# An RWKV block on one core: six block projections by seven products each, and a variance in the unused strip of another matmul

## The chip, the core and the metric

The kernel runs on one core of a Trainium2 chip. The core has TensorE (PE, matrix products into PSUM; its weight loads are listed apart as PEld), VectorE (DVE), ScalarE (ACT), GpSimd (POOL), and SyncE (SP), which here issues nearly all DMAs. The metric is the time of one execution in microseconds of the device, as the median of several runs. A lower number is better.

## The reference

There are 8 batches of 256 tokens (T) with 512 channels (E), in 32 heads of 16. Everything is float32. The part that matters:

```python
xn = _ln(x, ln1_w, ln1_b);  sx = _token_shift(xn, state[:, i1])
xxx = tanh((xn + sx * maa_x) @ maa_w1);  x5 = xn + sx * (maa_stack + xxx @ maa_w2)
w = exp(-exp(time_decay + tanh(x5[1] @ decay_w1) @ decay_w2))
r, k, v = x5[3] @ Wr.T, x5[0] @ Wk.T, x5[2] @ Wv.T;  g = silu(x5[4] @ Wg.T)
def step(s, rkvw):                      # over the 256 tokens
    a = k_t[..., None] * v_t[..., None, :]
    out = einsum('bhk,bhkd->bhd', r_t, u * a + s);  return a + w_t[..., None] * s, out
att = ((a4 - m) * rsqrt(var + EPS)).reshape(b, l, E) * gn_w + gn_b   # per head
x = x + att * g @ Wo.T
xn2 = _ln(x, ln2_w, ln2_b);  sx2 = _token_shift(xn2, state[:, i0])
xk = xn2 + sx2 * ffn_maa_k;  xr = xn2 + sx2 * ffn_maa_r
x = x + sigmoid(xr @ ffn_Wr.T) * (square(relu(xk @ ffn_Wk.T)) @ ffn_Wv.T)
```

## The kernel before

Each batch passes three stages: `inputs_of_scan` (normalize, shift, mix, project to k, v, r, g and the decay w), `scan`, and `rest` (normalize per head, output projection `o`, second normalization, and the three projections of the feed-forward part: `fk`, `fr`, `fv`). Most tiles hold channels on the 128 partitions and tokens along the free axis, two blocks of 128 channels to a tile, so 512 channels are two tiles, called halves here (q = 0, 1 in the code).

The scan of a batch has four channel blocks of four tiles of 128 x 1024 each. For every tile a DMA spreads v over the partitions (`vs`, six buffers), DVE multiplies it by k (L864) and runs the recurrence (L866), POOL multiplies by r (L869), and PE gathers the sums over the state (L877). DVE adds the result to `att` (L883). That is 128 tiles over all batches, and the scans of the batches follow each other almost without a break; the projections of the batches before and after lie beside them.

All matmuls of projections are issued by the helper `mul` (L330), as one 128-column matmul for each block of contraction or as four of 32 columns side by side in the array. `project` gives channels on the partitions, `project_tokens` tokens. A whole projection is a product of 512 x 512 by 512 x 256. In the trace every float32 matmul instruction makes two records.

After the scan, `rest` squares `att` (L895), and PE averages the squares of each head (L903): four matmuls into four column strips of one tile. ACT turns the variance into its inverse root by a logarithm and an exponential (L908, L910). The 32 heads' values must then be spread over 128 partitions. In batches 0 to 6 ACT does it by sixteen copies of 32 rows (L932); in batch 7 PE does it by a matmul with a 0/1 matrix (L918). `att` is multiplied by it (POOL, L934; in batch 7 DVE, L926), scaled by `gn_w` and `gn_b` on ACT (L938) and multiplied by g (L943; in batch 7 L941). The output projection follows, and DVE adds it to x (L949). After the second normalization (L493, L467, L499, transposed by PE at L525) come `fk`, `fr` and `fv`; in batch 7 the last 256 columns of the result are made in two pieces of 128 (L983, L985), each sent out by its own DMA.

The strip matmul at L741 is part of `inputs_of_scan`: in the four 32-column strips of the array, strips 0 and 1 compute the decay's hidden layer, and strips 2 and 3 compute the hidden layer of the fifth mix twice, since its `tanh` (L749) is wanted on all partitions.

The weights of `o`, `fk`, `fr` and `fv` are loaded again for every batch, each as two tiles of the pool `Ws` (four buffers). PSUM has six buffers for matmuls (`ps`) and one wide one (`wrep`).

The order of all instructions is not that of the code. Every operation is recorded in a plan, and a long list of numbers (`ORDER`) says in which order they are emitted; each engine then runs its instructions strictly in that order. Buffers are given out along the list too.

Of the kernel before, what the change touches and what calls it, by code (L numbers as in the profile page):

```python
# [11 lines left out]
P = 128  # L12
# [24 lines left out]
C_SEL = C_SUM + P  # L37
NCONST = P + C_SEL + 2 * P

# [21 lines left out]

class Op:


    def __init__(self, engine, us, outs, ins, emit, mode):
        self.engine, self.us, self.emit, self.mode, self.narrow, self.table = engine, us, emit, mode, False, None
        self.bufs = list(dict.fromkeys([*outs, *ins]))
        self.before, self.wire = [], 0


class Plan:
# [1024 lines left out]
```

## Time and profile before

| | |
|---|---|
| median of 3 runs | 602.61 us (601.87 to 603.97) |
| profiled execution | 603.54 us, its span 601.7 us, mean TensorE clock 0.996 |
| matmuls and weight loads | 8308 each |
| DMA | 128.07 MB, 211 GB/s of HBM traffic over the span |

The span runs from the first to the last instruction in the profile. The granted clock is the share of TensorE's full clock that the throttle let pass. Groups of instructions are listed with their count, their busy time, the mean duration of one in ns, and the engine's idle time before them.

### The profile page before, as it was taken

How to read it: one execution, taken by the hardware profiler on the slowest of the kernel's cores; microseconds unless marked ns; L12 is line 12 of the kernel's file. 1: busy time of each engine (PE TensorE's matmuls, PEld its weight loads, DVE VectorE, ACT ScalarE, POOL GpSimd, SP SyncE). 2: the span in 40 equal slices, each digit the busy share in tenths (PEclk: the TensorE clock that was granted, in tenths of full speed). 3: DMA queues.
4: the chain of work that ended last, by engine and by line, in shares of the span. 5: the costliest groups of instructions: out<-in, count | busy, mean ns of one | idle time of the engine just before them, and what ended most of it. 6: DMA issues, size and time to landing. Idle time of an engine off the chain costs nothing.

```text
span 601.7 us, 19771 instructions
## 1 busy us (share of the span) xinstructions
PE 592.1 (98%) x8308; PEld 343.5 (57%) x8308; DVE 537.5 (89%) x500; ACT 504.9 (84%) x1198; POOL 507.2 (84%) x390
## 2 busy tenths in 40 slices
PE   8999998999999999999999999999999999999997
PEld 7575556457536775366553754465645574455464
DVE  5799999999999999899889999999999999996342
ACT  5898779899999999989999988989987879964531
POOL 0689999899989999999979898999798999888030
PEclk9999999899999999999999999999999999999999
DMA  8797768887888869778888897687899887952533
GB/s 295 228 246 196 186 155 246 239 221 203 224 229 246 221 163 276 220 203 230 203 250 221 224 251 212 163 234 206 219 257 242 214 234 206 280 180 73 189 122 109
DMA packets 55497, 128.07 MB, mean 213 GB/s; under 512 B 6112, under 2 KB 13680, under 8 KB 55408
## 3 DMA queue, kind: packets, MB, share of 16 engines
q1 hardware_dynamic: 51040, 122.61, 74.9%
q10 hardware_dynamic: 4368, 4.20, 2.2%
q8 instruction: 65, 1.06, 0.8%
q14 instruction: 24, 0.20, 0.1%
HBM read 118.39 MB, written 8.40 MB: 211 GB/s over the span
## 4 chain that ended last, share of the span: by engine, by line
PE 83%; POOL 10%; ACT 2%; DVE 2%; issue 2%; DMA 0%; SPq 0%; POOLq 0%; ACTq 0%
PE ps L330 70%; PE ps L877 8%; POOL st L869 5%; POOL mix L701 3%; PE ps L741 2%; PE ps L525 2%; POOL vs L861 1%; DVE st L493 1%; POOL rk L814 1%; PE ps L903 1%; DMA sq<-in_x 0%; POOL mix L569 0%; PE ps L819 0%; POOL att L833 0%; POOL mix L729 0%
## 5 line engine op out<-in xcount | busy, mean ns | idle before, releaser
L866 DVE TENSOR_TENSOR_SCAN st<-wrep,vs 128x1024 f32<-128x1024 f32 x128 | 288.2, 2277 | 2.2 <-POOL mix L701 0.6
L869 POOL TENSOR_TENSOR st<-st,r 128x1024 f32<-128x1024 f32 x128 | 254.7, 2002 | 8.3 <-DVE st L866 5.1
L864 DVE TENSOR_TENSOR vs<-vs,ps 128x1024 f32<-128x1024 f32 x125 | 147.7, 1208 | 6.1 <-ACT vs L857 4.1
L330 PE MATMUL ps<-Ws,mix 128*32 128x512 f32 (+3 forms) x836 | 115.5, 585 | 0.0
L330 PEld LDWEIGHTS ps<-Ws,mix 128*32 128x32 f32 (+1 forms) x836 | 39.0, 118 | 61.9 <-issue 54.6
L701 POOL TENSOR_TENSOR mix<-mix,xn 128x512 f32<-128x512 f32 x62 | 67.1, 1095 | 7.1 <-DVE mix L695 4.1
L330 PE MATMUL ps<-mix,Wv 128*32 128x256 f32 (+1 forms) x880 | 62.2, 389 | 2.1 <-POOL mix L701 2.1
L877 PE MATMUL ps<-st,con 128*32 128x256 f32 x1024 | 61.9, 380 | 0.0
L330 PE MATMUL ps<-mix,Wr 128*32 128x256 f32 (+1 forms) x760 | 60.7, 380 | 0.2 <-ACT v L772 0.2
L330 PE MATMUL ps<-mix,Wg 128*32 128x256 f32 (+1 forms) x904 | 60.4, 379 | 0.0
L330 PE MATMUL ps<-mix,Wk 128*32 128x256 f32 (+1 forms) x856 | 59.5, 380 | 0.0
L330 PE MATMUL ps<-mix,Ws 128*32 128x256 f32 (+1 forms) x928 | 57.5, 379 | 0.0
L330 PE MATMUL ps<-Ws,g 128*32 128x512 f32 (+1 forms) x464 | 56.9, 592 | 0.5 <-POOL g L943 0.5
L569 POOL TENSOR_TENSOR mix<-mix,xn 128x512 f32<-128x512 f32 x44 | 47.5, 1091 | 7.3 <-ACT mix L567 7.3
L330 PEld LDWEIGHTS ps<-mix,Wv 128*32 128x32 f32 (+1 forms) x880 | 39.8, 117 | 22.0 <-issue 4.4
L330 PEld LDWEIGHTS ps<-mix,Wr 128*32 128x32 f32 (+1 forms) x760 | 39.5, 119 | 17.2 <-issue 1.1
L827 ACT COPY att<-ps 32x256 f32<-32x256 f32 x128 | 46.5, 364 | 2.7 <-PE ps L819 0.5
L330 PEld LDWEIGHTS ps<-mix,Wg 128*32 128x32 f32 (+1 forms) x904 | 37.2, 114 | 18.9 <-issue 1.0
L330 PEld LDWEIGHTS ps<-mix,Wk 128*32 128x32 f32 (+1 forms) x856 | 38.5, 115 | 16.6 <-issue 1.2
L877 PEld LDWEIGHTS ps<-st,con 128*32 128x32 f32 x1024 | 34.4, 110 | 23.6 <-issue 2.8
L330 PEld LDWEIGHTS ps<-mix,Ws 128*32 128x32 f32 (+1 forms) x928 | 35.9, 113 | 20.3 <-issue 1.2
L689 ACT ACTIVATE ps<-ps,vec 128x256 f32<-128x256 f32 x112 | 44.3, 449 | 3.5 <-PE ps L330 3.1
(134 smaller groups left out, 940.0 us busy)
## 6 DMA issues: line engine op xcount, KB each, us to landing
vs<-vo SPq DMA_DIRECT2D x128, 512.0 KB, 5.9
Ws<-in_fk SPq DMA_DIRECT2D x16, 512.0 KB, 6.2
Ws<-in_fr SPq DMA_DIRECT2D x16, 512.0 KB, 5.2
Ws<-in_wo SPq DMA_DIRECT2D x16, 512.0 KB, 5.9
Ws<-in_fv SPq DMA_DIRECT2D x16, 512.0 KB, 4.9
x<-in_x SPq DMA_DIRECT2D x11, 512.0 KB, 6.3
vo<-v ACTq DMA_DIRECT2D x15, 256.0 KB, 3.7
out<-o SPq DMA_DIRECT2D x15, 256.0 KB, 5.3
```

The costliest lines, as they stand in the source:

```text
L330: nc.tensor.matmul(out[i : i + n], lhsT=w[:, i : i + n], rhs=x, start=first, stop=final)
L493: dve(512, [st], [s], lambda st=st, s=s: nc.vector.bn_stats(out=st(), in_=s()))
L525: nc.tensor.transpose(ps()[:, m, n * P : (n + 1) * P], xh[n]()[:, k * P : (k + 1) * P], idt())
L569: gp(512, t, [t, xn[q]], lambda q=q, t=t: nc.gpsimd.tensor_tensor(t(), t(), xn[q]()[:, :, 1 : T + 1], ALU.add))
L689: act(256, p_, [p_, vec], lambda g=g, q=q, m=m, p_=p_: nc.scalar.activation(p_()[:, m, :], p_()[:, m, :], AF.Identity, bias=col(f"maa_{g}" ...
L701: gp(512, t, [t, xn[q]], lambda q=q, t=t: nc.gpsimd.tensor_tensor(t(), t(), xn[q]()[:, :, 1 : T + 1], ALU.add))
L741: nc.tensor.matmul(pd()[i : i + 32, 0, :], lhsT=w, rhs=src[k // 2]()[:, k % 2, :], start=(k == begin), stop=(k == end))
L827: act(350, atts[q], [pc], lambda i=32 * (2 * q + m), m=m, q=q, h=32 * h: nc.scalar.copy(atts[q]()[h : h + 32, m, :], pc()[i : i + 32, 0, :]))
L864: dve(4 * T, [vs], [vs, kp], lambda m=m, vs=vs, kp=kp: nc.vector.tensor_tensor(vs(), vs(), kp()[:, m : m + 1, :].to_broadcast([P, 4, T]), ...
L866: dve(4 * T, [st], [w, vs], lambda w=w, vs=vs, st=st: nc.vector.tensor_tensor_scan(st().rearrange("p n t -> p (n t)"), w().rearrange("p n ...
L869: gp(4 * T, st, [st, r], lambda m=m, st=st, r=r: nc.gpsimd.tensor_tensor(st(), st(), r()[:, m : m + 1, :].to_broadcast([P, 4, T]), ALU.mul ...
L877: nc.tensor.matmul(pat()[32 * i : 32 * i + 32, 0, :], lhsT=con()[:, s : s + 32], rhs=done[i]()[:, j, :], start=(j == 0), stop=(j == 3),)
```

## The change

1. **Seven products.** For six projections (`o`, `fk`, `fr`, `fv` of batch 7 and `fr`, `fv` of batch 6) both factors are cut into 2 x 2 blocks, and the result is made of seven block products in place of eight (Strassen's scheme in Winograd's form). It takes four block sums of each factor, made by POOL (in advance for the weights), and the products are put together on DVE, which reads them from PSUM; ACT copies the first product out of PSUM. One block product is 256 x 256 by 256 x 128 (or the same with the roles exchanged).
2. **Kept weights.** `fr` and `fv` of batch 6, and their block sums, are kept for batch 7: the weights in four of the scan's `vs` tiles, the sums in tiles of k, r, v, w and of `st8`.
3. **Variance in a strip.** For batches 1 to 5 the averaging of squares moves into strip 3 of the strip matmul of the batch two later. The fifth mix's hidden layer is then computed once and its `tanh` written by four instructions of 32 rows in place of two of 64. The inverse root is taken on 32 rows x 512 for each half and copied three times to the other rows, in place of sixteen copies.
4. **Batch 7's spreading** by PE (L918) becomes the sixteen ACT copies, here into PSUM.
5. The head masks move from four DVE instructions to one on POOL. The last output pieces become blocks of 256 columns, and two of 128.
6. A new `ORDER` list.

```diff
+SHARED = (3, 4, 5, 6, 7)
+SEVEN = {"o7": "vs", "fk7": "st8", "fr7": "krvw", "fv7": "st8", "fr6": "krvw", "fv6": "st8"}
+KEPT = {"fr", "fv"}
...
     ORDER = """
-        38 37 2 0 22 23 39 41 40 42 43 44 14 15 46 45 16 17 363 47 24 3 471 4 144 9 691 6 8 10 1 7 5 11 57 31 25 34
...
+    def seven(name, w, src, tokens=True):
...
+        for out, x, y, how in ((0, a[1, 0], a[1, 1], ALU.add), (1, s[0], a[0, 0], ALU.subtract),
+                               (2, a[0, 0], a[1, 0], ALU.subtract), (3, a[0, 1], s[1], ALU.subtract)):
+            if s is xs or not ready:
+                tensor("POOL", ns, s[out], x, y, how)
+        for out, x, y, how in ((0, b[0, 1], b[0, 0], ALU.subtract), (1, b[1, 1], t[0], ALU.subtract),
+                               (2, b[1, 1], b[0, 1], ALU.subtract), (3, t[1], b[1, 0], ALU.subtract)):
+            if t is xs or not ready:
+                tensor("POOL", nt, t[out], x, y, how)
+        pairs = {1: (a[0, 0], b[0, 0]), 2: (a[0, 1], b[1, 0]), 3: (s[3], b[1, 1]), 4: (a[1, 1], t[3]),
+                 5: (s[0], t[0]), 6: (s[1], t[1]), 7: (s[2], t[2])}
...
+        one = product(1)
+        act(256, old[0], [one], lambda: nc.scalar.copy(old[0](), one()))
+        tensor("DVE", T, old[1], product(6), old[0], ALU.add)
+        tensor("DVE", T, old[2], product(5), old[1], ALU.add)
+        return product, one, *old
...
+    def results(product, one, old, six, five, less, split=False):
+        r = {(1, 0): product(4), (0, 1): product(3), (1, 1): product(7)}
+        tensor("DVE", T, less, six, r[1, 0], ALU.subtract)
+        tensor("DVE", T, r[0, 1], five, r[0, 1], ALU.add)
+        tensor("DVE", T, r[1, 0], less, r[1, 1], ALU.add)
+        tensor("DVE", T, r[1, 1], five, r[1, 1], ALU.add)
+        if not split:
+            r[0, 0] = product(2)
+            tensor("DVE", T, r[0, 0], old, r[0, 0], ALU.add)
+        return r
...
+                        elif i == DEC or not shares:
+                            w, src = w1()[:, k, P : P + MAA], xin[k // 2]()[:, k % 2, :]
+                        else:
+                            w, src = con()[:, C_MEAN : C_MEAN + 32], older["sq"][k // 2]()[:, k % 2 * T : k % 2 * T + T]
+                            first, final, to = True, True, pvs[k // 2]()[i : i + 32, k % 2, :]
+                        nc.tensor.matmul(to, lhsT=w, rhs=src, start=first, stop=final)
...
+        if "pv" in got:
+            for q in range(NQ):
...
+                for i in range(3):
+                    act(512, sqs[q], [sqs[q]], lambda q=q, i=i, rows=rows: nc.scalar.copy(
+                        sqs[q]()[32 * i : 32 * i + 32], sqs[q]()[rows]))
...
-                        nc.tensor.matmul(
-                            pr[q]()[:, m, :], lhsT=con()[rows, s : s + P], rhs=rs()[rows, 0:T], start=True, stop=True)
...
+            rsb = new("ps", f"psr{b}_{q}") if last else sqs[q] if "pv" in got else new("rk", f"rsb{b}_{q}") if q else sqs[1]
...
+        if f"o{b}" in SEVEN:
+            added(blocks, *seven(f"o{b}", Wo, ys))
```

`added` puts the products of `o` straight into the blocks of x, one or two additions on DVE for each product. Line numbers of the changed kernel are higher: 330 becomes 355 (`mul`), 741 becomes 881, 877 becomes 1020, 903 becomes 1054, 895 becomes 1031, 932 becomes 1069, 938 becomes 1074.

Three places in the order. The first is PE just before the scan of batch 7, at the strip matmul of that batch. Before, strips 2 and 3 are both `mw` (the fifth mix) rows:

```order
L741 MATMUL ps_177<-mix_120,dw_69 32x256 x2
L741 MATMUL ps_177<-mix_111,mw_66 32x256 x2
L741 MATMUL ps_177<-mix_120,dw_69 32x256 x2
L741 MATMUL ps_177<-mix_111,mw_66 32x256 x2
L741 MATMUL ps_177<-mix_112,dw_69 32x256 x2
```

In the changed kernel:

```order
L881 MATMUL ps_174<-mix_112,dw_69 32x256 x2
L881 MATMUL ps_174<-mix_121,mw_66 32x256
L881 MATMUL ps_174<-sq_162,con 32x256
L881 MATMUL ps_174<-mix_112,dw_69 32x256 x2
L881 MATMUL ps_174<-mix_121,mw_66 32x256
L881 MATMUL ps_174<-sq_162,con 32x256
```

One of the two `mw` rows has become a row with `con` and the squares of batch 5 (`sq`), in the same place; the strip matmul has no more rows than before, and the four rows of L903 for batch 5 are gone elsewhere.

The second place is PE after the last gather of the last scan, up to the output projection of batch 7. Before (`g` rows further down are that projection, `Ws,mix` of 512 columns are `fr` of batch 6, L903 the variance and L918 the spreading of batch 7):

```order
L330 MATMUL ps_176<-Ws_170,mix_110 32x512 x8
L903 MATMUL ps_177<-sq_162,con 32x256 x2
L903 MATMUL ps_177<-sq_163,con 32x256 x2
L330 MATMUL ps_174<-Ws_170,mix_110 32x512 x8
L918 MATMUL ps_173<-sq_162,con 128x256
L918 MATMUL ps_177<-sq_162,con 128x256
L918 MATMUL ps_173<-sq_162,con 128x256
L918 MATMUL ps_177<-sq_162,con 128x256
L330 MATMUL ps_176<-Ws_171,mix_118 128x512 x2
L330 MATMUL ps_174<-Ws_171,mix_118 128x512 x2
L330 MATMUL ps_175<-Ws_168,g_139 128x512 x2
L330 MATMUL ps_175<-Ws_169,g_138 128x512 x2
```

In the changed kernel two products of the sevens of batch 6 stand ahead of the variance (L1054), and then:

```order
L1054 MATMUL ps_175<-sq_162,con 32x256 x2
L1054 MATMUL ps_175<-sq_163,con 32x256 x2
L355 MATMUL ps_178<-mix_108,Ws_170 32x256 x8
L355 MATMUL ps_178<-mix_114,Ws_169 32x256 x8
L355 MATMUL ps_175<-r_129,mix_118 32x256 x8
L355 MATMUL ps_178<-mix_108,Ws_170 32x256 x8
L355 MATMUL ps_178<-mix_114,Ws_169 32x256 x8
L355 MATMUL ps_175<-mix_108,Ws_170 32x256 x8
L355 MATMUL ps_175<-mix_114,Ws_169 32x256 x8
L355 MATMUL ps_175<-mix_108,Ws_170 32x256 x8
L355 MATMUL ps_175<-mix_114,Ws_169 32x256 x8
L355 MATMUL ps_174<-Ws_171,g_138 32x256 x8
```

Between the variance and the first product with `g` now stand nine stretches of two blocks of contraction over 256 columns: eight of `fk` of batch 6 (`Ws` read with `mix`) and one product of a seven (`r`, a kept block sum of weights). The spreading matmul is gone, and the projection itself follows in 256-column products: three that read g itself, then four with POOL's sums of it.

The third place is ACT at the same time, from the square of the second half of `att` on. Before:

```order
L895 ACTIVATE sq_163<-att_142 128x512
L1019 ACT_TABLE_LOAD
L908 ACTIVATE sq_162<-ps_177,few 128x256
L910 ACTIVATE sq_162<-sq_162 128x256
L958 ACTIVATE mix_108<-ps_175 128x512
L938 ACTIVATE att_141<-att_141,vec 128x256 x2
L938 ACTIVATE att_142<-att_142,vec 128x256 x2
L958 ACTIVATE mix_121<-ps_178 128x512
```

In the changed kernel:

```order
L1031 ACTIVATE sq_163<-att_142 128x512
L1202 ACT_TABLE_LOAD
L1059 ACTIVATE sq_162<-ps_175,few 128x256
L1061 ACTIVATE sq_162<-sq_162 128x256
L1069 COPY ps_174<-sq_162 32x256
L1069 COPY ps_176<-sq_162 32x256
L1069 COPY ps_174<-sq_162 32x256
L1069 COPY ps_176<-sq_162 32x256
L1069 COPY ps_174<-sq_162 32x256
```

The copies go on to sixteen in all, alternating between the two PSUM tiles, and then come the four scalings by `gn_w` and `gn_b` (L1074), first those of one half, then those of the other. Before, the scalings followed two instructions behind the exponential, with PE's spreading and DVE's multiply between.

More of the change, by code (lines that the diff above doesn't have):

```diff
@@ L59, in __call__, with __init__ @@
         return self.view(self.buf())
+class Half(Part):
+    def __init__(self, buf, view):
+        super().__init__(buf, view)
+        self.writers, self.readers, self.before = [*buf.writers], [], set()
+class Group:
+    def __init__(self, parts, view):
+        self.parts, self.view = parts, view
+    def __call__(self):
+        return self.view()
 class Op:
@@ L425, in load_x @@
         return pieces([t])
+    kept = {}
     def stream(name, src, b):
-        tiles = [new("Ws", f"W{name}{b}_{h}") for h in range(2)]
+        if name in KEPT and b == NB - 1:
+            return kept[name]
+        keeps = name in KEPT and b == NB - 2
+        tiles = [new("vs" if keeps else "Ws", f"W{name}{b}_{h}") for h in range(2)]
+        if keeps:
+            for t in tiles:
+                t.view = lambda t: t.rearrange("p (k j) t -> p k (j t)", k=2)
+            kept[name] = pieces(tiles)
         load_pairs(tiles, src)
@@ L597, in project_tokens, with halves, tensor @@
         return ps
+    def halves(pool, name, n, width):
+        each = {"mix": 2 * T, "st8": 4 * T, "vs": 4 * T}[pool] // (2 * width)
+        tiles = [new(pool, f"{name}{i}") for i in range(-(-n // each))]
+        return [Half(tiles[i // each], lambda t, j=i % each * 2 * width: t.rearrange("p m t -> p (m t)")[:, j : j + 2 * width]
+                     .rearrange("p (k w) -> p k w", k=2)) for i in range(n)]
+    def tensor(engine, n, out, a, b, how):
+        if engine == "DVE":
+            dve(n, [out], [a, b], lambda: nc.vector.tensor_tensor(out(), a(), b(), how))
+        else:
+            gp(n, out, [a, b], lambda: nc.gpsimd.tensor_tensor(out(), a(), b(), how))
@@ new lines, in added @@
+    def added(blocks, product, one, old, six, five, less):
+        x_ = blocks[0, 0]
+        dve(T, [x_], [x_, one, six], lambda: nc.vector.tensor_tensor(x_(), x_(), one(), ALU.add))
+        r = {(1, 0): product(4), (0, 1): product(3), (1, 1): product(7)}
+        tensor("DVE", T, r[1, 0], six, r[1, 0], ALU.subtract)
+        tensor("DVE", T, blocks[1, 0], blocks[1, 0], r[1, 0], ALU.add)
+        tensor("DVE", T, blocks[1, 0], blocks[1, 0], r[1, 1], ALU.add)
+        for i in ((0, 1), (1, 1)):
+            tensor("DVE", T, r[i], five, r[i], ALU.add)
+            tensor("DVE", T, blocks[i], blocks[i], r[i], ALU.add)
+        tensor("DVE", T, blocks[0, 0], blocks[0, 0], product(2), ALU.add)
@@ L733, in inputs_of_scan @@
         pd, hd = new("ps", f"psd{b}"), new("w", f"w{b}_0")
+        shares = b in SHARED
+        if shares:
+            older["pv"] = pvs = [pd, new("ps", f"psd{b}_")]
         for ks in turns:
@@ L939, in rest @@
                     att()[:, m, :], att()[:, m, :], AF.Identity, bias=col("gn_b", blk), scale=col("gn_w", blk)), None, 2)
[L940 to L943 removed]
+            tensor("DVE" if last else "POOL", 2 * T, g, att, g, ALU.mult)
             ys.append(g)
@@ L962, in rest @@
         Wfr = stream("fr", fr, b)
-        os = []
-        for n in range(NT):
+        os, outs = [], {}
+        if f"fr{b}" in SEVEN:
+            os = [new("o", f"o{b}_{n}") for n in range(NT)]
+            outs = {(n, c): Half(os[n], lambda t, c=c: t[:, c * T : (c + 1) * T]) for n in range(NT) for c in range(2)}
+            for i, r in results(*seven(f"fr{b}", Wfr, xr)).items():
+                act(256, outs[i], [r], lambda t=outs[i], r=r: nc.scalar.activation(t(), r(), AF.Tanh, scale=HALF), "tanh")
+        for n in range(NT if not os else 0):
             o = new("o", f"o{b}_{n}")
@@ L970, in rest @@
         Wfv = stream("fv", fv, b)
+        if f"fv{b}" in SEVEN:
+            product, one, *old = seven(f"fv{b}", Wfv, kk)
+            if last:
+                y, x_ = outs[0, 0], blocks[0, 0]
+                dve(T, [one], [y, one], lambda: nc.vector.scalar_tensor_tensor(one(), y(), 1.0, one(), ALU.add, ALU.mult))
+                tensor("DVE", T, x_, x_, one, ALU.add)
+                two = [product(2, slice(h * P, (h + 1) * P)) for h in range(2)]
+            for i, t in results(product, one, *old, last).items():
+                o, t2 = outs[i], blocks[i]
+                dve(T, [t], [o, t], lambda o=o, t=t: nc.vector.scalar_tensor_tensor(t(), o(), 1.0, t(), ALU.add, ALU.mult))
+                tensor("DVE", T, o, t, t2, ALU.add)
+                if last:
+                    n, cols = i[0], slice(i[1] * T, (i[1] + 1) * T)
+                    dma(None, lambda o=o: o(), lambda n=n, cols=cols: out[b, n * P : (n + 1) * P, cols], 131, o)
+            if last:
+                for h, t in enumerate(two):
+                    o = Half(outs[0, 0].buf, lambda t, h=h: t[:, h * P : (h + 1) * P])
+                    o.writers = [*outs[0, 0].writers]
+                    o.readers = [*outs[0, 0].readers]
+                    t, x_ = Part(t.buf, lambda t, h=h: t[:, 0, h * P : (h + 1) * P]), Group([blocks[0, 0]], lambda h=h: blocks[0, 0]()[:, h * P : (h + 1) * P])
+                    dve(P, [t], [o, t], lambda o=o, t=t: nc.vector.scalar_tensor_tensor(t(), o(), 1.0, t(), ALU.add, ALU.mult))
+                    tensor("DVE", P, o, t, x_, ALU.add)
+                    dma(None, lambda o=o: o(), lambda h=h: out[b, 0:P, h * P : (h + 1) * P], 66, o)
+            else:
+                for n in range(NT):
+                    dma(None, os[n], lambda n=n: out[b, n * P : (n + 1) * P, :], 256, Group([outs[n, c] for c in range(2)], os[n]))
+            return
         for n in range(NT):
@@ L1010, in tile_rwkv_block @@
     centered_weights()
-    for b in range(NB):
-        got = {}
-        for stage in (inputs_of_scan, scan, rest):
-            stage(b, got)
+    got = [{} for _ in range(NB)]
+    for b in range(NB + 2):
+        if b < NB:
+            inputs_of_scan(b, got[b], got[b - 2] if b > 1 else None)
+        if 0 < b <= NB:
+            scan(b - 1, got[b - 1])
+        if b > 1:
+            rest(b - 2, got[b - 2])
     with tc.manual_schedule():
```

162 lines of the change are left out of this document (98 added, 64 removed), and 236 rows, old and new, of the table ORDER.

## The prediction

> **What bounds the kernel now.** I read the page first: the span, the busy shares and the engines in the chain that ended last.
>
> ```profile
> span 601.7 us, 19771 instructions
> PE 592.1 (98%) x8308; PEld 343.5 (57%) x8308; DVE 537.5 (89%) x500; ACT 504.9 (84%) x1198; POOL 507.2 (84%) x390
> PE 83%; POOL 10%; ACT 2%; DVE 2%; issue 2%; DMA 0%; SPq 0%; POOLq 0%; ACTq 0%
> ```
>
> PE is busy almost throughout and is most of the chain, but a share over the whole span hides stages. So I cut the span by windows at three places: 104.7 us, where the chain leaves POOL for PE, 554 us, where the last scan's gather ends, and 25 us.
>
> ```profile
> core 0: us, PE busy (x) PEld busy (x) DVE busy (x) ACT busy (x) POOL busy (x), PEclk, DMA share, GB/s
> 0.00:25.00 25.00, 21.80 (x261) 17.77 (x265) 17.07 (x46) 16.18 (x40) 7.00 (x18) 1.00 0.80 273
> 25.00:104.70 79.70, 77.46 (x1340) 49.22 (x1332) 75.58 (x69) 67.89 (x158) 75.89 (x55) 1.00 0.81 205
> 104.70:554.00 449.30, 448.74 (x6544) 252.44 (x6548) 429.48 (x357) 402.05 (x969) 418.25 (x312) 1.00 0.81 217
> 554.00:601.70 47.70, 44.09 (x176) 24.11 (x168) 15.39 (x30) 18.75 (x33) 6.10 (x6) 0.99 0.46 153
> ```
>
> In the long middle PE idles 0.6 of 449.3 us, so PE work removed there is time, as long as DVE follows: it is busy 429.48, or 96%, and idles 19.8. In the last 47.7 us DVE, ACT and POOL have room (15.4, 18.8 and 6.1 busy), and PE alone is full. The one long pause of PE stands at the border of the first stages; the first row is the timeline of PE, the second a window.
>
> ```profile
> 104.68 5.35 PE L330 MATMUL ps<-mix,Wv 128*32 128x256 f32 x64 [2.05 <-POOL mix L701]
> 104.70:110.00 5.30, 5.30 (x68) 2.92 (x72) 5.30 (x5) 5.11 (x12) 5.00 (x4) 0.68 1.01 306
> ```
>
> PE waits 2.05 us for POOL there, and the granted clock then is 0.68 for 5.3 us, which loses 0.32 x 5.3 = 1.7 us more. Before this point POOL's queue sets the pace, and POOL has the same kinds and number of long instructions ahead of it after the change; I count the first 104.7 us as unchanged (bounds: 1.7 us of clock won if the pause is cut up, 1.7 lost if a second one comes).
>
> **The change part by part.** First the PE work, from the timeline (PE) and the chain of waits (rows with no operation name).
>
> ```profile
> 8.36 1.95 PE L330 MATMUL ps<-Ws,Ws 128*128 128x128 f32 x16
> 577.56 7.09 PE L330 MATMUL ps<-mix,Ws 128*128 128x256 f32 x32
> 584.49 13.97 PE L330 MATMUL ps<-Ws,mix 128*128 128x512 f32 x48
> 432.03 0.43 PE ps L903 x8
> 459.03 1.73 PE ps L741 x32
> 555.68 0.43 PE ps L903 x8
> 557.83 1.06 PE ps L918 x8
> ```
>
> A whole projection (ffn_k of batch 7) lasts from 577.56 to the next at 584.49: 6.93 us, or 0.866 for each of eight block products. Seven in place of eight save 0.87 in six projections: 5.2. The ffn_k of batch 7 is built from 128-column pieces; 16 records of that width took 1.95 us, 0.12 each, against 7.09 / 64 = 0.11 per 128 columns in the wide form. Its 28 products of two records each so give back about 0.2 (bounds 0 and 56 x 0.01 = 0.6). The variance of batches 1 to 5 goes into strip 3 of a strip matmul that runs anyway (L741, 1.73): 5 x 0.43 = 2.2. The spreading matmul L918 goes: 1.06. **PE work: -5.2 + 0.2 - 2.2 - 1.06 = -8.2 us.** Does the strip now wait? In batch 7 it starts at 459.03, and L903 of batch 5, whose squares it needs, ran at 432.03; so these are 27 us old. The new wait ends before.
>
> Now the end. The rows are the timeline from the last gather on, and the groups that price the new steps.
>
> ```profile
> 552.06 1.91 PE L877 MATMUL ps<-st,con 128*32 128x256 f32 x32
> 556.95 0.42 ACT L910 ACTIVATE sq<-sq 128x256 f32<-128x256 f32 x1
> 562.37 7.03 PE L330 MATMUL ps<-Ws,g 128*128 128x512 f32 x16
> 569.43 0.69 DVE L949 TENSOR_TENSOR x<-ps,x 128x512 f32<-128x512 f32 x1 [2.68 <-PE ps L330]
> 573.19 1.09 PE L525 MATMUL ps<-idt,xh 128*128 128x128 f32 x8 [0.36 <-DVE xh L499]
> 598.50 0.29 DVE L983 SCALAR_TENSOR_TENSOR sq<-o,ps 128x128 f32<-128x128 f32 x1 [0.28 <-PE ps L330]
> 598.82 0.29 DVE L985 TENSOR_TENSOR sq<-sq,x 128x128 f32<-128x128 f32 x1
> 503.19 1.23 ACT L932 COPY rk<-sq 32x256 f32<-32x256 f32 x3
> L938 ACT ACTIVATE att<-att,vec 128x256 f32<-128x256 f32 x32 | 17.7, 593 | 2.8 <-DVE att L926 1.9 <-POOL att L934 0.9
> L941 DVE TENSOR_TENSOR g<-att,g 128x512 f32<-128x512 f32 x2 | 1.4, 694 | 0.9 <-ACT att L938 0.9
> L883 DVE TENSOR_TENSOR att<-ps,att 128x256 f32<-128x256 f32 x32 | 13.3, 415 | 7.1 <-PE ps L877 6.8
> L827 ACT COPY att<-ps 32x256 f32<-32x256 f32 x128 | 46.5, 364 | 2.7 <-PE ps L819 0.5 <-POOL g L943 0.3
> L506 POOL TENSOR_TENSOR nm<-mn,rs 128x2 f32<-128x2 f32 x10 | 1.9, 194 | 17.0 <-ACT rs L469 16.9
> L943 POOL TENSOR_TENSOR g<-att,g 128x512 f32<-128x512 f32 x14 | 15.2, 1091 | 5.6 <-ACT att L938 5.6
> ```
>
> Call the gather's end S = 552.06 + 1.91 = 553.97. Up to the exponential nothing changes: it ends at 557.37, S + 3.4. Before, the output projection began at 562.37, S + 8.4. Now ACT makes sixteen copies of 32 rows in L918's place. Three took 1.23 us, so 0.41 each and 6.6 in all (bounds: 0.36, the copy L827 from PSUM, and 0.41). They end at S + 10.0. The first half's multiply on DVE runs beside the last copies; then two scalings on ACT (one each 0.5 us, 0.59 to the end of the second: 1.1) and the product with g (0.69): S + 11.8. What PE has until then is, by the new order, two products of the sevens, the variance and nine stretches of 0.866: 2 x 0.87 + 0.43 + 9 x 0.866 = 9.95. **PE waits 1.9 us.** The second half comes one us later, when the first product is over: 0.15 more.
>
> The next links have cover. The output projection's seven end at S + 11.8 + 7 x 0.866 + 0.15 = S + 18.0. Behind them DVE has six additions of 0.42 (2.5), and the statistics and normalization, 3.1 as from the end of L949 (570.12) to the transposes (573.19): 5.6. PE has six products beside them (5.2). What is left, 0.4, stands where 0.36 stood before. Then POOL must add blocks of the shifted input before the products of sums can start. A 256-column addition isn't in the trace; the bounds are 0.2 (POOL's two-column instructions) and 1.09; I take 0.58, half the 512-column row and a little. Four products of batch 6 and two of batch 7 lie beside them; going through the chain I find 0.2 uncovered. POOL's sums are 16 x 1.09 + 24 x 0.58 = 31 us in all, nearly all of it after S, where 41 are free. DVE gets some 45 instructions of 0.42 more and 13 fewer: 15.4 busy becomes about 30 of 47. If these covers failed, each link would cost its own 1 to 3 us; that is the upper end of the range.
>
> At the very end the 128-column piece (0.29 + 0.29 behind PE) becomes an addition, a multiply and two more additions of 256 columns: 4 x 0.42 against 0.6, **1.1 us longer**; the output piece is 128 KB in place of 64, whose landing the next rows show to be alike (KB each, then us).
>
> ```profile
> out<-o SPq DMA_DIRECT2D x1, 128.0 KB, 1.7
> out<-sq SPq DMA_DIRECT2D x2, 64.0 KB, 1.6
> L463 DVE TENSOR_SCALAR hm<-con,vec 128x32 f32<-128x32 f32 x4 | 2.4, 595 | 0.0
> L1019 ACT ACT_TABLE_LOAD x34 | 43.6, 1283 | 1.0 <-ACT v L772 0.4
> L749 ACT ACTIVATE tb<-ps 64x256 f32<-64x256 f32 x16 | 6.1, 380 | 0.8 <-PE ps L741 0.5
> ```
>
> Counted at nothing: the head masks (2.4 us of DVE at 23 to 32 us, now one POOL instruction of about 0.4 while POOL is idle, bounds -1 and +1); ACT's three more table loads (3.8) and ten more tanh (3.8), against 16 copies a batch that become six wide ones (about 1.3 saved in each of five batches): 1 us of ACT on 402 busy of 449; four weight loads fewer, where the DMA share is 0.46.
>
> **Sum:** -8.2 + 1.9 + 0.15 + 0.2 + 1.1 = -4.85 us. Against the profiled execution (603.54, its span 601.7) that is 598.7; against the median of the runs, 0.9 below that execution, **597.8 us**.
>
> **A rule weighed.** The row: after 2.05 us of waiting the clock was 0.68 for 5.3 us. The Trainium skill, "TensorE: Matmul & The Clock Gate", Part 1, says that the clock is halved after an idle window of some 3.4 us, and that the window runs freely. By that rule a wait of 1.9 us is too short to matter, and the sum stays 597.8; the trace differs, since one of 2.05 us was followed by the loss, so the row makes 599.5 possible. One pause doesn't tell how often that happens; I leave it out of the sum and keep it as a rival.
>
> **The rivals.** *DVE binds the middle (slower).* The change takes nothing from DVE between 104.7 and 554. For PE's saving to arrive, the scan must end g = 7.6 us earlier (8.2, less 0.6 that falls behind it: PE had 598.50 - 553.97 = 44.5 us there and has 50.5 x 0.866 + 0.2 = 43.9), and DVE's idle shrink from 19.8 to 12.2. That idle is made of waits on others:
>
> ```profile
> DVE att L883 <- PE ps L877: 3.0, 4, 1.7
> DVE mix L691 <- ACT ps L689: 2.8, 4, 1.3
> 50.00:75.00 25.00, 24.82 (x468) 14.72 (x460) 25.00 (x19) 20.94 (x50) 24.99 (x17) 1.00 0.79 195
> 75.00:100.00 25.00, 24.99 (x494) 15.69 (x490) 25.00 (x25) 20.32 (x45) 24.79 (x18) 1.00 0.70 191
> ```
>
> If the new order keeps it, the time is 602.6 - 0.6 + 3.35 - g = 605.4 - g. At g = 0 it is 605.4; it is slower for g under 0.9 and faster for g over 4.5. For it: DVE is 96% busy already, and the kept weights take four of the scan's six input tiles before the last scan is over. Against it: from 50 to 100 us DVE ran without idle (the two windows), so it can run full. *The new wait drops the clock*, as at 104.7: 1.7 more, 599.5; the wait is as long as that one, but where it falls in the gate's time is chance. *The wait doesn't come*, if the copies go at 0.3 or the half that is needed first is ready sooner, 595.8; without the early pause's clock loss too, 594.1. *The products don't save*, if block sums stall each of the six: that needs more than 0.87 each, 603.0; it speaks against it that the products which need no sum of the late factor stand first in the order. I count it with DVE's middle values.
>
> **Numbers.** Forecast 0.56; no wait 0.14; clock 0.10; DVE's (or the products') middle values, g from 0.9 to 4.5, 0.12; slower 0.08. Faster by over 0.3% (which a measurement here can just tell from none; below 600.8) is 0.56 + 0.14 + 0.10 = 0.80; within it 0.12; slower (above 604.4) 0.08. The range 594.0 to 602.6 leaves out the slow case, the half of the middle values above 602.6, and a little below.
>
> **What would show it.** PE records of L741's successor holding the variance; six projections at 6.05 to 6.3 us of PE; a wait of about 1.9 us of PE for DVE's product with g, some 11 us behind the last gather; DVE's idle near 12 us between 104.7 and the scan's end; some 4.3 us between the last matmul and the span's end, for 3.2 now. I am wrong if the scan's end moves by less than 4 us, or if PE pauses at several of the six.

## The result and the profile after

The changed kernel takes **609.25 us** (median of four runs, 608.05 to 610.04) against 603.15 for the kernel before (four runs): a ratio of 1.0101, with a 95% interval of 1.0074 to 1.0129. It is 1% slower, where 597.8 us was forecast. The profiled execution of it took 608.05, its span 606.3.

First the page of the changed kernel: the span, the busy shares, and the engines of the chain that ended last.

```profile
span 606.3 us, 20316 instructions
PE 590.5 (97%) x8500; PEld 342.8 (57%) x8500; DVE 555.2 (92%) x549; ACT 516.3 (85%) x1201; POOL 543.7 (90%) x429
PE 70%; ACT 10%; DVE 7%; POOL 7%; issue 4%; DMA 2%; SPq 0%; ACTq 0%; POOLq 0%; DVEq 0%
```

PE looks as full as before, for the ends of matmuls are modelled and a PE that is fed late shows little of it. The chain tells more: PE fell from 83% to 70% of it, and ACT rose from 2% to 10%. Next the windows of the changed kernel, cut as before, with the end of the last gather now at 551.0.

```profile
core 0: us, PE busy (x) PEld busy (x) DVE busy (x) ACT busy (x) POOL busy (x), PEclk, DMA share, GB/s
0.00:25.00 25.00, 21.08 (x236) 17.99 (x240) 15.73 (x43) 15.48 (x37) 5.77 (x17) 0.93 0.78 259
25.00:104.70 79.70, 78.63 (x1379) 47.50 (x1372) 73.63 (x68) 67.24 (x159) 76.25 (x58) 1.00 0.80 202
104.70:551.00 446.30, 443.22 (x6374) 240.12 (x6370) 430.51 (x357) 406.17 (x945) 420.87 (x314) 1.00 0.83 221
551.00:606.30 55.30, 47.58 (x534) 37.20 (x522) 35.33 (x83) 27.38 (x62) 40.86 (x44) 0.96 0.25 82
```

Three things differ from the forecast. In the first 25 us the clock is 0.93, where it was 1.00. The scan ends 3.0 us earlier (553.97 to 551.0), not 7.6. From there to the end it takes 55.3 us; the forecast had 596.85 - 546.4 = 50.5, and before it was 47.7. So of the 9.45 us by which the span misses the forecast (606.3 against 596.85), 4.6 lie ahead of the scan's end and 4.85 behind it. The list of what PE waited for in the changed kernel (total, number of waits, longest):

```profile
PE ps L560 <- DVE xh L534: 2.6, 2, 2.0
PE ps L355 <- DVE g L643: 1.9, 2, 1.8
PE ps L355 <- POOL g L645: 1.1, 2, 0.8
```

The second row is the wait that was forecast. The first, at the start (2.0) and in the tail (0.5), was 1.2 in the kernel before. The third is the tip of something larger in the middle.

A busy PE can hide waits, so I also count its work, as an estimate: a record of 256 columns over the whole array costs 6.93 / 32 = 0.217 us, by the projection that the prediction priced, and other records go by their columns and their part of the array. The sum is 575.5 us before and 567.3 after. So the 8.2 us of work are saved as forecast, and the whole miss is time in which PE is not at work, with what a lower clock costs counted in. This table has that time by stage; a stage ends where a batch's last gather begins. (The row of e12 belongs to the end of the experiments.)

| PE not at work, us | up to batch 0 | batch 0 to 1 | batch 1 to 7 | from batch 7 on | sum |
|---|---|---|---|---|---|
| before | 10.4 | 5.7 | 6.0 | 4.2 | 26.2 |
| changed | 13.4 | 1.4 | 11.7 | 12.4 | 39.0 |
| e12 | 11.9 | 1.5 | 10.8 | 7.1 | 31.2 |

### The profile page after: what moved, and what is told of

It is laid out like the page before. It is cut to its first block, busy times and chain, and to the rows that moved or that the text cites. A ratio compares the mean times of both kernels' runs of the same rounds, so it can differ in the third digit from the quotient of the medians.

```text
span 606.3 us, 20316 instructions
## 1 busy us (share of the span) xinstructions
PE 590.5 (97%) x8500; PEld 342.8 (57%) x8500; DVE 555.2 (92%) x549; ACT 516.3 (85%) x1201; POOL 543.7 (90%) x429
## 4 chain that ended last, share of the span: by engine, by line
PE 70%; ACT 10%; DVE 7%; POOL 7%; issue 4%; DMA 2%; SPq 0%; ACTq 0%; POOLq 0%; DVEq 0%
PE ps L355 59%; PE ps L1020 7%; DVE st L1009 3%; ACT sq L1046 2%; PE ps L881 2%; PE ps L560 1%; POOL st L645 1%; POOL mix L645 1%; POOL st L1012 1%; DMA Ws<-in_wo 1%; POOL g L645 1%; DVE vs L1007 1%; ACT ps L1069 1%; ACT sq L1041 1%; ACT sq L1043 1%
## 5 line engine op out<-in xcount | busy, mean ns | idle before, releaser
L355 PE MATMUL ps<-Ws,mix 128*32 128x512 f32 (+1 forms) x784 | 89.1, 589 | 0.0
L355 PE MATMUL ps<-mix,Wv 128*32 128x256 f32 (+1 forms) x904 | 59.3, 380 | 1.0 <-DVE att L1026 0.9
L355 PE MATMUL ps<-mix,Ws 128*32 128x256 f32 (+1 forms) x920 | 56.1, 377 | 0.7 <-DVE mix L597 0.6
L355 PE MATMUL ps<-Ws,g 128*32 128x512 f32 (+1 forms) x480 | 52.5, 587 | 3.3 <-DVE g L643 1.8
L355 PEld LDWEIGHTS ps<-Ws,mix 128*32 128x32 f32 x784 | 25.8, 110 | 47.7 <-issue 40.3
L355 PEld LDWEIGHTS ps<-mix,Wk 128*32 128x32 f32 (+1 forms) x880 | 37.1, 114 | 20.1 <-issue 2.2
L355 PEld LDWEIGHTS ps<-mix,Wv 128*32 128x32 f32 (+1 forms) x904 | 36.6, 113 | 20.4 <-DVE att L1026 1.8
L355 PEld LDWEIGHTS ps<-mix,Wg 128*32 128x32 f32 (+1 forms) x832 | 36.8, 116 | 19.3 <-issue 1.0
```

The source lines that it names most:

```text
L355: nc.tensor.matmul(out[i : i + n], lhsT=w[:, i : i + n], rhs=x, start=first, stop=final)
```

## The experiments

Twelve kernels ran in four groups, each group beside the kernel before on the same chip. All ratios are to the kernel before, whose medians in the groups are 603.36, 603.42, 603.48 and 603.75 us. Where two intervals overlap, the difference of the times alone proves little, and the places in the profiles decide.

| run | what | us | ratio | 95% interval |
|---|---|---|---|---|
| changed | | 609.25 | 1.0101 | 1.0074 to 1.0129 |
| e1 | batch 7's spreading on PE again | 607.81 | 1.0082 | 1.0064 to 1.0100 |
| e2 | second half's load first | 606.49 | 1.0060 | 1.0044 to 1.0076 |
| e3 | no copies in batches 1 to 5 | 604.63 | 1.0040 | 1.0021 to 1.0059 |
| e4 | own variance in batches 1 to 5 | 615.52 | 1.0209 | 1.0192 to 1.0226 |
| e5 | e1, and o7, fk7 plain | 605.94 | 1.0037 | 1.0022 to 1.0051 |
| e6 | e1, and all six plain | 617.45 | 1.0232 | 1.0185 to 1.0279 |
| e8 | e1 and e2 | 605.60 | 1.0040 | 1.0024 to 1.0057 |
| f1 | before, with fr7 as seven | 602.48 | 0.9977 | 0.9965 to 0.9989 |
| e9 | e2, no copies in 1 to 3 | 604.55 | 1.0014 | 1.0000 to 1.0027 |
| e10 | e2, no copies in 4 and 5 | 605.69 | 1.0038 | 1.0025 to 1.0052 |
| e11 | e6, DVE's order mended | 608.82 | 1.0083 | 1.0061 to 1.0105 |
| e12 | e2 and e5 together | 604.05 | 1.0012 | 0.9998 to 1.0027 |

### The start: one load past another (e2)

The list `ORDER` of the change begins 34 2 35: half of x, the vectors, the other half. SP issues loads in that order. The timeline of DVE in the changed kernel, then its window from 8 to 12 us:

```profile
3.54 0.69 DVE L528 BATCH_NORM_STATS2 st<-sq 128x6 f32<-128x512 f32 x1 [2.48 <-DMA sq<-in_x]
4.92 0.69 DVE L528 BATCH_NORM_STATS2 st<-sq 128x6 f32<-128x512 f32 x1 [0.68 <-DMA sq<-in_x]
```

```profile
8.00:12.00 4.00, 4.00 (x24) 4.00 (x23) 1.93 (x4) 2.55 (x7) 0.00 (x0) 0.59 1.08 384
```

DVE waits 0.68 us for the second half, PE then 2.0 us for the normalized halves, and the clock behind that wait is 0.59.

```diff
-        34 2 35 0 20 19 ...
+        34 35 2 0 20 19 ...
```

> The changed kernel with two loads in the other order: the second half of the first batch ahead of the vectors, as before. Theory 'the load order costs the start': DVE's statistics of the second half start at 4.2 us (4.9), PE's wait of 2.0 us for the normalized halves shrinks to about 1.3, the window of 8 to 12 us shows a clock of 1.00 (0.59), and the time falls by 1.4 to 2.2 us, to about 607.4. Rival 'the stages up to 100 us absorb it' (POOL and DVE set their pace): the first strip comes 1.4 us earlier, but the strip of batch 2 doesn't, and the time stays within 0.5 of 609.25.

Measured: 606.49, 2.8 us less, more than the 1.4 to 2.2 expected; between the two profiles the span differs by 1.1. In DVE's timeline of e2 the two statistics run back to back:

```profile
3.26 1.53 DVE L524 BATCH_NORM_STATS2 st<-sq 128x6 f32<-128x512 f32 x2 [2.19 <-DMA sq<-in_x]
```

One execution wouldn't settle it, since the start varies. But every run here has a profile. With the vectors first (seven kernels: changed, e1, e3, e4, e5, e6, e11) the first strip matmul starts at 19.3 to 21.2 us, and in four of them PE waited 2.0 us or more (2.03, 2.40, 2.17, 2.92) and the clock fell to between 0.58 and 0.64 in 8 to 12 us; in the other three it waited 1.09 to 1.28, and the clock stayed. With the second half first (before, e2, e8, e9, e10, e12, f1) the strip starts at 18.5 to 19.2, the wait is 0.35 to 1.37, and the clock is 1.00 in all seven. (In e2 PE then waits 1.67 us for a load of weights, so its strip comes only 0.9 earlier.) The theory holds; the rival, that the stages up to 100 us absorb it, falls. Part of the gain in time is the chance of the clock.

### The tail's wait for g (e1, e8)

The timeline of PE in the changed kernel, from the output projection of batch 7 on:

```profile
562.93 1.07 PE L355 MATMUL ps<-Ws,g 128*32 128x256 f32 x16 [1.79 <-DVE g L643]
564.17 1.93 PE L355 MATMUL ps<-vs,g 128*32 128x256 f32 x16 [0.16 <-DVE g L643]
565.81 1.97 PE L355 MATMUL ps<-Ws,g 128*32 128x256 f32 x16
567.52 1.99 PE L355 MATMUL ps<-vs,mix 128*32 128x256 f32 x32
```

It starts 11.9 us behind the scan's end; 11.8 was forecast, and the waits of 1.79 and 0.16 are the 1.9 and the 0.15. The second and the third product last 1.93 and 1.97 in place of 1.07: the clock.

```diff
+            pe(0.945, pr, [con, rs], spread, "rows64")
-            for n in range(0 if "pv" in got else 2):
+            for n in range(0 if "pv" in got or last else 2):
```

> The changed kernel (609.25 us) with one thing undone: the last batch's variance is spread over the rows by the matmul of before (1.06 us on PE) in place of sixteen copies on ACT. The constants' load grows back by 126 KB. Theory 'the copies cost the tail 3.6 us': the output projection of batch 7 starts about 10.9 us behind the last gather (11.9 in the changed kernel), PE waits under 0.3 us for g there (1.95), the granted clock of the 6 us behind it is 0.95 or more (0.50 to 0.84), and the time falls by 1.0 + 1.7 = 2.7 us, to 606.6. Rival 'what is behind binds anyway' (POOL's sums of batch 7 and DVE's recombination): the wait comes back at the next link, and the time falls by less than 1 us.

Measured: 607.81, 1.4 us less, between the theory and its rival; the intervals overlap, but the profiles show the place. PE's timeline of e1:

```profile
562.18 1.03 PE L351 MATMUL ps<-Ws,g 128*128 128x256 f32 x4
563.40 1.10 PE L351 MATMUL ps<-vs,g 128*128 128x256 f32 x4 [0.19 <-DVE g L639]
```

The wait and the clock's loss are gone. From the last gather's first record to the span's end it takes 56.4 us (548.91 to 605.3), where it took 57.9 (548.35 to 606.3): 1.5 less, the theory's 1.0 for the wait and only 0.5 of its 1.7 for the clock, since the next links were not PE's (below). And the loss of clock is not the rule: the same wait of 1.8 us stands in e2, e3, e4, e9 and e10, and there the clock stayed at 1.00. e8 puts both mends together:

> Two mends at once: the spreading on TensorE (alone 607.81, 1.4 below the changed kernel) and the second half's load ahead of the vectors (alone 606.49, 2.8 below). If the two are apart, as their places at both ends of the span suggest, the gains add up: 605.1 within 0.8. If the start's gain is given back behind it, or was the chance of those four executions: 606.5 to 608.

Measured: 605.6. The start's gain is 2.2 on top of e1, so the two add up.

### The middle: the chain behind the strip (e3, e4, e9, e10)

The chain of waits of the changed kernel passes three times through the work that follows a strip, and comes back to PE at the output projections of batches 1 to 3. At the strips of batches 4 and 5 it comes from PE; at that of batch 3 it comes from ACT, which is still at earlier work until 178.0 us. This is the second of these places; the sum over the whole program follows as groups of ACT.

```profile
249.43 1.98 PE ps L881 x32
251.43 0.69 ACT sq L1041
...
259.32 0.62 ACT sq L1046
260.01 1.10 POOL att L645
261.20 1.10 POOL g L645
262.38 1.10 POOL g L645
263.52 4.48 PE ps L355 x37
```

```profile
L1046 ACT COPY sq<-sq 32x512 f32<-32x512 f32 x30 | 18.5, 616 | 0.6
L1041 ACT ACTIVATE sq<-ps,few 32x512 f32<-32x512 f32 x10 | 6.7, 678 | 2.0 <-PE ps L881 1.9
```

From the strip's end (251.4) to the projection (263.5) it takes 12.1 us, and PE is not always ahead enough to have other work for all of it: it waits for POOL's g 0.3 us in batch 1 and 0.8 in batch 3. The first experiment shortens this chain.

```diff
-                for i in range(3):
-                    act(512, sqs[q], [sqs[q]], lambda q=q, i=i, rows=rows: nc.scalar.copy(
-                        sqs[q]()[32 * i : 32 * i + 32], sqs[q]()[rows]))
```

> The changed kernel without the three copies of 32 rows by 512 for each half of batches 1 to 5 (so three quarters of the rows of their scale are not the variance's). ACT's chain from the strip to g is six instructions of 0.62, 3.7 us, shorter in each of five batches. Theory 'the variance in the strip makes the output projections of batches 1 to 5 wait': the scan's end comes 2 to 3 us earlier, and the time falls by as much, to about 606.7. Rival 'POOL and DVE bind the middle': the scan's end moves by less than 0.6, the time stays within 0.6.

Measured: 604.63, 4.6 us less than the changed kernel; in the profiles the scan's end comes 2.3 earlier, of which 0.8 stands already at the first strip, so 1.5 is left for the copies. The rest of the time is not theirs: behind the scan's end e3's profile gains another 1.1, where the changed kernel's lost its clock. The other direction, a variance of its own:

```diff
-SHARED = (3, 4, 5, 6, 7)
+SHARED = ()
```

> The changed kernel with the variance of batches 1 to 5 as a matmul of its own just ahead of the strip, and sixteen copies of 32 rows by 256 on ACT again in place of six of 512. PE has 5 x 0.43 = 2.2 us more work; ACT's chain starts 1.7 us earlier and the first half's scale is ready after 8 copies (3.3 us) from there. Theory 'the strip's late variance costs the middle 3 us': the loss in the middle falls by some 2, which pays for the matmuls, 609 within 0.8. Rival 'the strip saves its 2.2 and the loss is not its doing': 611.4.

Measured: 615.52, 6.3 us more; neither theory had that number. The reason is in e4's list of PE's waits:

```profile
PE ps L353 <- POOL g L643: 7.5, 4, 2.8
```

In my order POOL's scaling of the second half stood behind all sixteen copies, so the chain became longer, not shorter (the output projection of batch 2 starts 15.0 us behind the strip's start, 14.1 in the changed kernel). PE waits 7.5 us for g where it waited 1.1, and the 6.4 more are near the loss; the 2.2 us of added work, an earlier start and a tail that kept its clock stand beside them. It was not the test that I meant: it shows that a later g holds PE, and not what the strip's late variance costs.

Removing copies also takes work from ACT. So two more runs removed them in some batches only, on the base of e2:

```diff
-                for i in range(3):
+                for i in range(3 if b > 3 else 0):
```

> The run with the second half's load ahead (606.49 us), without the three copies for each half of batches 1 to 3 alone (three quarters of the rows of their scale are then not the variance's): 18 instructions of 0.62 on ACT less. Theory 'the chain from the strip to the output projection holds PE in batches 1 to 3', as the chain of the changed kernel shows at 178, 251 and 324 us: nearly all of what the removal in all five batches gave (1.9 us against this base), so 604.8. Rival 'ACT's load costs': three fifths of it, 605.4.

> The same base without the copies of batches 4 and 5 alone: 12 instructions of 0.62 on ACT less. Theory 'the chain in batches 1 to 3': no gain, 606.5 within 0.4. Rival 'ACT's load costs': two fifths of 1.9, 605.7.

Measured: 604.55 and 605.69, 1.9 and 0.8 below e2. The times alone split nearly as ACT's load would (three fifths and two fifths). The places don't. This table, from PE's timelines, has the start of the first strip, and of the last gather of a batch:

| | strip | batch 2 | 3 | 4 | 5 | 6 | 7 |
|---|---|---|---|---|---|---|---|
| e2 | 19.2 | 227.7 | 292.1 | 365.4 | 426.6 | 490.3 | 547.7 |
| e9 | 18.5 | 225.7 | 290.2 | 362.8 | 424.0 | 487.7 | 544.2 |
| e10 | 18.8 | 226.6 | 291.6 | 365.2 | 426.3 | 489.9 | 546.5 |

e9 gains on e10 in steps, 0.6, 0.5 and 1.0 between the first strip and 365 us, where the output projections of batches 1 to 3 stand, and nothing behind. PE's waits for POOL's g, 1.1 us in e10, are gone in e9. So the chain holds PE in batches 1 to 3.

e10 gains on e2 0.8, all of it behind 490 us, where the output projection of batch 5 stands. That is not the copies' doing: e9, which keeps the copies of batches 4 and 5, gains as much there (from 490.3 to 547.7 it is 57.4 us in e2; the same stretch is 56.5 in e9 and 56.6 in e10). PE's rows of that projection, first in e2, then in e9:

```profile
516.21 7.07 PE L351 MATMUL ps<-Ws,g 128*32 128x512 f32 x64 [0.74 <-DMA Ws<-in_wo]
```

```profile
512.70 7.05 PE L350 MATMUL ps<-Ws,g 128*32 128x512 f32 x64
```

In e2's profile PE waits there for a load of weights, which neither of the other two does. So the theory's 'no gain' for batches 4 and 5 holds in the profiles, and the 0.8 in the times, whose intervals overlap, is not shown to come from the chain. The copies cost 1.5 us by e3 and 2.0 by e9 against e10, all in batches 1 to 3; the medians of e9 and e10 are 1.1 apart.

### The tail's sums (e5, e6, e11)

In e1 PE had its g without a wait, and yet little more was won. The timeline of DVE there, then one row of POOL's:

```profile
559.84 3.42 DVE L639 TENSOR_TENSOR g<-att,g 128x512 f32<-128x512 f32 x2 [0.56 <-ACT att L1081]
573.02 2.50 DVE L530 TENSOR_SCALAR xh<-x,mv,rs 128x512 f32<-128x512 f32 x2
```

```profile
560.96 1.75 POOL L641 TENSOR_TENSOR vs<-Ws,Ws 128x512 f32<-128x512 f32 x1
```

The two products with g took 0.69 each before and take 3.42 together; the normalization took 1.00 and takes 2.50. POOL adds weights beside them without a pause, and its own instruction is longer too, 1.75 where its neighbours take 1.28. e5 takes the sums of two projections away:

```diff
-SEVEN = {"o7": "vs", "fk7": "st8", "fr7": "krvw", "fv7": "st8", "fr6": "krvw", "fv6": "st8"}
+SEVEN = {"fr7": "krvw", "fv7": "st8", "fr6": "krvw", "fv6": "st8"}
```

> The run with the spreading on TensorE (607.81 us) with two of the six projections, o and ffn_k of batch 7, as eight plain block products again, at the places of their seven; their 16 additions on POOL and their recombination on DVE go. PE gets 1.74 - 0.2 = 1.5 us more. Theory 'the sums hold the tail': POOL is full from 549 to 581 us there, and DVE's instructions with two operands in SBUF take 1.0 to 1.7 us beside it (the products with g 3.42 us for two, 1.39 before; the normalization 2.50 for two, 1.00 before). Without these sums they go back to the times of before, from the last gather's first piece to the span's end it takes 53 to 54 us (56.4), and the time falls by 2.5 to 3.5, to about 604.8. Rival 'the products are worth what they save': 1.5 us more, 609.3.

Measured: 605.94, 1.9 us less than e1, though PE has 1.5 us more to do. DVE's timeline of e5:

```profile
560.00 0.69 DVE L637 TENSOR_TENSOR g<-att,g 128x512 f32<-128x512 f32 x1 [0.56 <-ACT att L1079]
572.67 0.99 DVE L528 TENSOR_SCALAR xh<-x,mv,rs 128x512 f32<-128x512 f32 x2
```

The old durations are back. From the last gather's first record to the span's end it takes 54.7 us (548.98 to 603.7), against the 56.4 of e1; 53 to 54 was expected, so the theory holds with a smaller size. Next, the other four:

```diff
+SEVEN = {}
```

> As the run before it, with the other four projections (ffn_r and ffn_v of batches 6 and 7) plain too: PE gets 4 x 0.87 = 3.5 us more work, and the end is 1.1 us shorter behind the last matmul. Theory 'a seven pays where its sums have cover': these four stand off the chain for the most part, so the time rises again against the run with two plain, by 1 to 2.4 us. Rival 'no seven pays while POOL is full': it falls further or stays within 0.5.

Measured: 617.45, which says nothing on the sevens. PE's waits in e6 show why:

```profile
PE ps L551 <- DVE xh L525: 3.5, 3, 1.3
PE ps L346 <- DVE mix L588: 3.4, 3, 2.0
```

In my order DVE took the output of ffn_v of batch 6 ahead of batch 7's normalization, and waited there for PE. With that mended:

> The run with all six projections plain, whose DVE waited for ffn_v of batch 6 ahead of batch 7's normalization (617.45 us): DVE's products with that output, and POOL's sums, now stand behind the four mixes of batch 7. Theory 'the four sevens off the chain pay': 606.5 to 608, above the run with o and ffn_k plain (605.94). Rival 'no seven pays while POOL is full': 606.0 or less.

Measured: 608.82, 2.9 above e5 and above the expected range too. About 0.9 of it is the start (first strip 21.2 against 20.3). So the four sevens of ffn_r and ffn_v save some 2 us of the 3.5 that they take from PE, and the two of o and ffn_k lose 1.9.

### What adds up, and a version that beats both (e12, f1)

> The three mends that keep the computation whole, together: the second half's load ahead of the vectors, the spreading on TensorE, and o and ffn_k of batch 7 as eight plain products (605.94 us with the last two alone). If the start's share is apart from the tail's, as in the run with the first two (605.6 against 607.81), it falls by 2.2, to 603.7, level with the kernel of before within 0.3%; what is then left against the forecast is the chain behind the strip, worth 2 to 3 us by the runs without copies, and the sums' own pace. If the mends overlap: 604.7 or more.

Measured: 604.05, a ratio of 1.0012 (0.9998 to 1.0027). Three mends undo nearly the whole loss; the start's share is 1.9 here.

The last kernel is the one of before with a single seven, the one whose sums have cover on every side. As an edit to the code of the change, with the rest of the change taken back and the order of before:

```diff
-SEVEN = {"o7": "vs", "fk7": "st8", "fr7": "krvw", "fv7": "st8", "fr6": "krvw", "fv6": "st8"}
+SEVEN = {"fr7": "krvw"}
-SHARED = (3, 4, 5, 6, 7)
+SHARED = ()
-        keeps = name in KEPT and b == NB - 2
+        keeps = name == "fr" and b == NB - 1
```

> The kernel of before with one of the six projections alone as seven products: ffn_r of batch 7, whose weights go to two tiles of the scan, free by then, right behind the last scan, so that POOL makes the sums of weights while it has nothing else (6.1 of 47.7 us busy) and the sums of its input beside ffn_k. Nothing waits for it but the last projection. Theory 'a seven pays where its sums have cover': 0.87 us less, 602.5. Rival 'even there the sums or the recombination come late': 603.4 or more.

Measured: 602.48 us (twelve runs) against 603.42 (29), **0.9977 (0.9965 to 0.9989)**: faster than both kernels. The medians are 0.9 us apart, as was expected; the ratio makes it 1.4, with 0.7 to 2.1 as its interval. f1's profile kept its clock at 104.7 us, where the profile of before lost it, so the two profiles (2.5 us apart) say too much. But the gain is no luck of the clock: among the runs with a mean clock of 0.999 or more the medians are 601.30 for f1 (5 runs) and 602.20 for before (12), among the others 602.73 (7) and 603.86 (17). The timeline of PE in f1, then POOL's:

```profile
575.90 7.09 PE L349 MATMUL ps<-mix,Ws 128*128 128x256 f32 x32
582.83 1.89 PE L349 MATMUL ps<-vs,mix 128*128 128x256 f32 x8
...
588.88 7.11 PE L349 MATMUL ps<-Ws,mix 128*128 128x512 f32 x32
```

```profile
564.12 1.18 POOL L637 TENSOR_TENSOR w<-r,vs 128x512 f32<-128x512 f32 x1
573.42 1.04 POOL L577 TENSOR_TENSOR sx<-xn 128x512 f32<-128x512 f32 x1 [8.12 <-ACT xn L573]
584.74 0.73 POOL L637 TENSOR_TENSOR mix<-mix,mix 128x256 f32<-128x256 f32 x1
```

ffn_r takes 588.88 - 582.83 = 6.05 us in place of 6.93, without a wait. The sums of weights end at 565.3, 17 us before they are needed; POOL then idles 8 us while DVE normalizes; the sums of the input end 2.6 us into the projection, when the three products that need none of them are over.

## Why the prediction was wrong, point by point

- **"I count the first 104.7 us as unchanged": wrong.** I compared POOL's instructions there and did not read SP's queue, although the order showed it. One load moved past another made PE wait 2.0 us and cost it the clock: 1.9 to 2.8 us by e2, e8 and e12. And the pause of 2.05 us at 104.7 us with its loss of clock, which I carried over, is gone: PE is not at work 1.4 us between the last gathers of batches 0 and 1, where it was 5.7. Without that gain of 4.3 the miss would be larger. The bound that I gave, 1.7 for a second pause, was named and not followed up.
- **"The new wait ends before": wrong.** The squares are early, but that is only half of the question. I looked only at what goes into the strip, the squares, 27 us old. What comes out of it was late: the variance now waits for the strip, and ten instructions of ACT at 0.62 to 0.69 and three of POOL at 1.1 follow before the output projection. My "1 us of ACT on 402 busy" asked how much ACT has to do, not who waits for the last of it. The copies' share alone is 1.5 to 2.0 us, most of the 5 x 0.43 = 2.2 that the strip saved. From batch 1's last gather to batch 7's PE is not at work 5.8 us more than before; what is left of that beside the copies is not traced to a cause.
- **The rival "DVE binds the middle" had the symptom, not the cause.** The scan's end moved by 3.0, less than the 4 that I had set as the sign of being wrong, as in that rival's middle, and DVE idled 446.3 - 430.5 = 15.8 us there, between the 12 of the forecast and the 19.8 of before. But in e9 DVE has the same work as in e10, and the last gather starts at 544.2 in place of 546.5, only 0.3 of it won at the start. DVE followed.
- **The wait for g: right to 0.1 us**, in place, size and cause. Its price by e1, 0.9 to 1.4 us, is near the sum's 1.9 + 0.15 - 1.06 = 1.0.
- **"Wait drops the clock", kept as a rival of 0.10: it happened in the profiled execution** (the clock was 0.65 from 563 to 567), and in one of six profiles with this wait. To leave it out of the sum was right.
- **"Going through the chain I find 0.2 uncovered": wrong.** Two prices were too low, 1.28 against 1.09 for a sum of 512 columns and 0.73 against 0.58 for one of 256: 16 x 1.28 + 24 x 0.73 = 38 us in place of 31. POOL was busy 40.9 of the 55.3 us behind the scan. The other half I did not have at all: beside those sums DVE's products with g and its normalization took 2.5 times as long. For o and ffn_k of batch 7, which stand on the chain, both cost more than the 1.5 us that PE saves: 1.9 on top, 3.4 in all by e5, the largest loss that a run isolates. The text had the right bound ("each link would cost its own 1 to 3 us") and the wrong middle.
- **A rule that I had not weighed.** The Trainium skill, "SBUF — State Buffer", under "SBUF: two separate sides", says that DVE and GpSimd share one pair of ports under an exclusive lock, taken for a whole instruction, when a DVE instruction has two SBUF inputs or runs in a two-port mode. The runs agree: the product with g (two SBUF inputs) took 0.69 alone and 1.7 beside the sums, and DVE's additions with an operand in PSUM took 0.42 beside them as ever.
- **Six sevens of 0.87 each: right as a price, wrong as a sum.** f1 shows 0.88 on PE and 0.9 in time for one that has cover.
- **The end, "some 4.3 us": right.** The last matmul's record ends at 600.12 + 1.89 = 602.0, the span at 606.3.

What stays open: e12 is still 6.3 us above the forecast, and 1.1 of it is the kernel before, which took 603.75 beside it and not the 602.61 that I had counted from. In e12's profile, the fastest of its runs, the span of 601.1 is 4.25 above the forecast's 596.85. Of this 2.6 is PE work that was put back, the two plain projections and the spreading. By the table of PE's time not at work the start costs 1.5 more than before and the middle 4.8 more, the pause at 104.7 us saves 4.2, and the tail is near the forecast. The copies explain 1.5 to 2.0 of the middle. For the other 3 us I have no cause. It is not the sevens that are left: e11, which has none, is not at work 12.0 us in the middle, and e5, which has four, 12.2.

## What to carry to other kernels

Before a result is moved into an instruction that runs anyway, follow what waits for the result, not only what the instruction waits for: merged work is ready when the latest of it is. Saving PE work by additions on POOL pays where these additions and the recombination stand beside other work, and loses where they sit on the chain, also by what they do to DVE beside them. And read every queue of a new order from its first row, SP's too.

## What the runs showed of the hardware

Waits of PE well under 3 us were followed by a lower clock, but not always. At the start four waits of 2.03 to 2.92 us cost the clock (0.58 to 0.64 over 8 to 12 us), and ten of 0.35 to 1.37 did not. The same wait of 1.8 us in the tail cost it in one of six profiles. The wait of 2.05 us at 104.7 us is in both of these kernels; the windows behind it, first before, then f1:

```profile
104.70:108.00 3.30, 3.30 (x40) 1.83 (x44) 3.30 (x4) 3.18 (x9) 3.00 (x2) 0.62 1.03 348
```

```profile
104.70:108.00 3.30, 3.30 (x64) 1.99 (x66) 3.30 (x4) 3.18 (x9) 3.08 (x3) 1.00 0.96 335
```

The same pause, and a clock of 0.62 or 1.00. Cut at its own bounds, the loss in the kernel before is one stretch of 3.4 us at a clock of 0.50, and 0.62 is a mean that takes in its surroundings. The window ahead of it and the stretch itself:

```profile
102.11:105.52 3.41, 1.36 (x26) 0.58 (x22) 3.41 (x3) 3.33 (x10) 3.03 (x3) 1.00 0.95 262
105.52:108.94 3.42, 3.42 (x38) 1.74 (x32) 3.42 (x3) 3.26 (x9) 3.42 (x3) 0.50 1.03 314
```

Ahead of the last matmul the profiles have eight such stretches (before, e1, e5 and e11 one each, changed and e6 two), all of 3.4 us at 0.50, and in the 3.4 us ahead of each PE was busy 1.1 to 1.5 us. The Trainium skill, "TensorE: Matmul & The Clock Gate", Part 1, lets the clock fall after an idle window of about 3.4 us that runs freely. A free window of that length fits these rows, and the chance would follow from it if a pause falls into one window or is split between two. That the window must be idle does not fit, since PE was busy for a third of it or nearly half.

ACT's copies of 32 rows took 0.62 us for 512 columns and 0.40 for 256, so two narrow ones cost more than a wide one. The wide ones lost by where they stood, not by their price.
